# Short key tile split over the halves of a fast block product, in an attention and feed-forward kernel

## The chip, the core and the metric

The kernel runs on one core of a Trainium2 chip. The core has a matrix engine (TensorE, PE in the profile, with its weight loads as PEld), a vector engine (VectorE, DVE), a scalar engine (ScalarE, ACT), GpSimd (POOL) and SyncE (SP), which here only issues transfers. The engines run their own instruction queues in order and wait for one another through semaphores. The metric is the device time of one execution in microseconds, given as the median of several runs.

## The reference

For each of 4 batches there are 256 tokens of width 512 in x and 1601 rows of context of the same width. All data are fp32.

```python
xn = layernorm(x)
q = xn @ Wq + bq                     # 32 heads of 128
k, v = split(ctx @ Wkv + bkv)        # 8 key/value heads of 128; 4 query heads share one
attn = softmax(q @ k.T / sqrt(128))  # over the 1601 context rows
x = x + tanh(g_xattn) * ((attn @ v) @ Wo + bo)
h = layernorm(x)
x = x + tanh(g_ffn) * (h @ base_W.T + 2 * routed_lora(h))   # 8 experts, top 2, rank 16
```

1601 rows are twelve full tiles of 128 and a short one of 65. That short tile is what the change is about.

## The kernel before, in words

**Units.** The loop at the end of `flamingo_kernel` goes over batches `b` and key/value heads `h` (0 to 7) and, inside, over the two halves `l` of the 256 tokens. One such triple is a unit. `run_group(cur, prev)` writes the score matmuls of the current unit (`score_unit`, L799, tile `sc`, one matmul of 512 columns for each of 13 context tiles) alternately with the products of the previous unit's probabilities with the values (`av_unit`, L877, tile `av`). ScalarE copies each score tile from PSUM to SBUF (L806, tile `p`), VectorE keeps a running maximum (`fold`, tile `mx`, L731, L734 and L737) and later a running sum of the exponentials (tile `sm`).

**Softmax.** After a unit's scores, `softmax` reduces the maximum over partitions (`spread`: L769, L770, L750, L756, L757, L761, L764), then VectorE subtracts it from each pair of score tiles (L835) and ScalarE takes the exponential (L838). The first pair is the short tile alone. The first `av` matmul of the unit needs its exponential. The sums of the unit before are reduced by the same `spread` just ahead, and the result scales `av` to `oT` (L926, L930).

**Windows.** Between two units the function `window` puts other work on TensorE: query projections (`q_steps`, L480, `pq`), the output projection of a finished unit (`out_steps`, L942, `po`), key projections, value projections, context transposes (L226, `pt_ctx`) and the feed-forward steps. Each is a `Task`, a list of steps with costs, a time at which a step may start, and for some a due unit. A small clock in the kernel's own code (`clock`, `vec`, `act`, `later`, `pump`) estimates, with fixed figures for VectorE and ScalarE, when a result is ready; from these figures it decides at build time which step goes into which window and in which order VectorE and ScalarE get their instructions. The order of TensorE, VectorE and ScalarE is written out by hand this way (`manual_schedule`).

**Keys and values.** Keys and values of two heads are made together. `pair_steps` uses seven products of 2x2 blocks in place of eight: the context is cut into halves of 768 rows and each of the two heads' weights into blocks, and VectorE makes sums of context blocks (`ctx_sums`, L441, tile `T`, and `last_sums`, L452 and L456) once a batch. GpSimd makes the sums of the weights (`weight_sums`, L291). Each half is worked in two parts of 384 columns (`SUB`). The products of one part go to three PSUM banks (`pxk`, `pyk`, `pzk` for keys at L587, `pxv`, `pyv`, `pzv` for values at L598); between products ScalarE copies a bank out (L622, L626) and VectorE adds another bank to what was copied (L631). The short tile does not fit in the halves and has products of its own (L685, `ptk` and `ptv`).

The first pair of heads of every batch gets its keys by `plain_k_steps` (L512, `pk`): four chunks of 400 or 401 columns for each head, four matmuls a chunk. In batches 1 to 3 these steps lie in the last three windows of the batch before, and `last_sums` follows them.

**Buffers.** The context, its sums, the values and the weights of the output projection (`wo`) have one buffer each; the keys (`kT`) have three. `load_wo` for the next head is called in `out_steps` after the projection of a head's second half, since only then its buffer is free. The key and value weights share one buffer. SyncE issues the loads in the order of its queue.

Of the kernel before, what the change touches and what calls it, by code (L numbers as in the profile page):

```python
# [15 lines left out]
P = 128  # L16
# [11 lines left out]
def flamingo_kernel(  # L28
# [49 lines left out]

    nc = tc.nc
# [19 lines left out]
    n_chunks = -(-LK // 512)  # L99
    base, extra = divmod(LK, n_chunks)  # L100
# [3 lines left out]
    TAIL = 2 * HK  # L104
    chunks, s = [], 0
    for i in range(n_chunks):
        n = base + (1 if i < extra else 0)
        chunks.append((s, n))
        s += n
# [232 lines left out]
    xa_t, xnT_t, ctxT_t, T_t = {}, {}, {}, {}  # L342
# [40 lines left out]
    ctx_order += range(TAIL // P, KT)  # L383

    def ctx_steps(b):
# [9 lines left out]
        def begin():  # L395
            ctxT_t[b] = pool.tile([P, NC, LK], F32, tag="ctxT", name=f"ctxT_{b}", bufs=1)
            new_sums(b)

        def step(n):
            def run():  # L400
                i = ctx_order[n]
                if n + STAGE - 1 < KT:
                    load(n + STAGE - 1)
                turn_ctx(b, i, staged.pop(i))
                if n % 2 == 1 and i < TAIL // P:
                    ctx_sums(b, i * P - HK, P)
                if n == KT - 1:
                    done["ctx", b] = clock["now"] + 1000
            return NC * TR_COST, LAG_CTX, run, True
# [10 lines left out]
    def new_sums(b):  # L420
        t = pool.tile([P, 6 * HK + 2 * (LK - TAIL)], F32, tag="T", name=f"T_{b}", bufs=1)
        T_t[b] = (
            t[:, : 6 * HK].rearrange("p (n c k) -> p n c k", n=3, c=2),
            t[:, 6 * HK :].rearrange("p (c k) -> p c k", c=2),
        )

    def ctx_sums(b, s0, n):
# [3 lines left out]
        lo, hi = slice(s0, s0 + n), slice(HK + s0, HK + s0 + n)  # L431
# [12 lines left out]
    def last_sums(b):  # L444


        ct, tt = ctxT_t[b], T_t[b][1]
        for s0 in range(0, HK, SUB):
            b12, b22 = (ct[:, c : c + 2, HK + s0 : HK + s0 + SUB] for c in (0, 2))
# [6 lines left out]
            lambda: nc.vector.tensor_tensor(tt, ct[:, 2:4, TAIL:], ct[:, 0:2, TAIL:], ALU.subtract),  # L456
# [3 lines left out]
    def turn_ctx(b, i, src):  # L460
        transpose_rows(
            src,
            rows[i],
            ctxT_t[b][:, :, i * P : i * P + rows[i]],
            f"ctx_{b}_{i}",
            b > 0 or i % 2 == 1,
        )
# [37 lines left out]

    def plain_k_steps(b, h):

        def item(s, n):
            def run():
                pk = bank(f"pk_{b}_{h}_{s}")  # L510
                for c in range(NC):
# [3 lines left out]
                        ctxT_t[b][:, c, s : s + n],  # L515
# [3 lines left out]
                nc.scalar.activation(  # L519
                    kT_t[b, h][:, s : s + n], pk[:, :n], AF.Identity, bias=bias_of("k", h)  # L520
                )
                give(act(500))
            return NC * mm_cost(n), 0, run, True

        steps = [item(s, n) for s, n in chunks]
        return [(0, ("ctx", b), lambda: new_kT(b, h))] + steps

    def plain_v_steps(b, hp):
# [3 lines left out]
        def item(i):  # L532
# [3 lines left out]
            def run():  # L536
                w = w_t["v", b, hp]
                pv = bank(f"pv_{b}_{hp}_{i}")
                for j in range(n):
                    s = (i + j) * P  # L540
                    for c in range(NC):
# [3 lines left out]
                            ctxT_t[b][:, c, s : s + r],  # L545
# [12 lines left out]
    def pair_steps(kind, b, hp):  # L558
# [10 lines left out]
        def operand(i, c, s, n):  # L569
# [6 lines left out]
            if i == 3:  # L576
                return ct[:, 2 + c, HK + s : HK + s + n]
            if i == 7:
                return ct[:, c, HK + s : HK + s + n]
# [4 lines left out]
        def product(i, s, bk, first):  # L584
            if is_k:
                for c in range(2):
                    nc.tensor.matmul(  # L587
                        bk[:, :SUB],
                        a(SLOT[i], c),
                        operand(i, c, s, SUB),  # L590
# [16 lines left out]
        def place(f, half, s):  # L607

            if is_k:
                lo = half * HK + s  # L610
                return kT_t[b, h0 + f][:, lo : lo + SUB]
            lo = (half * HK + s) // P
            return v_t[b, hp][:, lo : lo + SUB // P, f, :]

        def seen(bk):
            if is_k:
                return bk[:, :SUB]
            return bk[:, :SUB].rearrange("p (t f) -> p t f", f=HDIM)

        def copy_to(f, half, s, bk):  # L620
            if is_k:
                nc.scalar.activation(  # L622
                    place(f, half, s), seen(bk), AF.Identity, bias=bias_of("k", h0 + f)
                )
            else:
                nc.scalar.copy(place(f, half, s), seen(bk))  # L626
            return act(470)

        def add_to(f, half, s, bk, ready=None):
            o = place(f, half, s)  # L630
            nc.vector.tensor_tensor(o, seen(bk), o, ALU.add)  # L631
            return vec(520, ready)

        def step(i, s):
# [3 lines left out]
            def run():  # L638
# [4 lines left out]
                product(i, s, bk, i in (1, 2, 7))  # L643
                if i == 1:
                    done[key] = done[nm, s, "x0"] = copy_to(0, 0, s, bk)
                elif i == 2:
                    give(add_to(0, 0, s, bk, max(clock["now"] + SEM, done[nm, s, "x0"])))
                elif i == 6:
                    done[key] = copy_to(1, 0, s, bk)
                elif i == 5:  # L650
                    done[key] = copy_to(1, 1, s, bk)
                    done[nm, s, "y"] = add_to(1, 1, s, banks[nm, s, "y"], done[key])
                elif i == 3:
                    give(copy_to(0, 1, s, bk))
                elif i == 4:
                    give(add_to(1, 0, s, bk))

            cost = 2 * (mm_cost(SUB) if is_k else SUB // P * BLOCK_COST)
# [5 lines left out]

        n = LK - TAIL

        def tail_cols(f):

            ct, tt = ctxT_t[b], T_t[b][1]
# [675 lines left out]
```

## Time and profile before

The median of three runs is 2690.46 us (2688.22 to 2691.63). One execution was profiled:

| | |
|---|---|
| profiled execution, its own time | 2691.11 us |
| its span, first to last instruction | 2689.3 us |
| mean granted TensorE clock | 0.995 |
| VectorE busy, ScalarE busy | 2151.5 us, 1199.3 us |
| scores, `sc`, L799 | 777.2 us in 1664 records |
| `av`, L877 | 769.5 us in 1640 records |
| plain keys, `pk`, L512 | 91.3 us in 256 records |
| short key tile, `ptk`, L685 | 24.7 us in 192 records |

How to read it: an fp32 matmul leaves two records. A row of the group list gives the line in the kernel, the engine, the operation, the tile written and the tiles read, the form (weight block, then partitions by columns), the count, the busy time and mean time of one, and the idle time of the engine before it with the one that released it. Matmul records overlap, so the time from one start to the next is shorter than a record. A row of the timeline gives start, length, engine, line, operation and how many records were merged.

### The profile page before, as it was taken

What the parts mean: (1) busy time and instruction counts of PE and PEld (TensorE: products, weight loads), DVE (VectorE), ACT (ScalarE), POOL (GpSimd) and SP (SyncE); (2) the same over time, 40 slices, a digit from 0 to 9 for tenths busy, and PEclk for the clock granted to TensorE, in tenths of its full rate; (3) what the DMA queues carried; (4) which work ended last, traced back from release to release, by engine and by line L of the source; (5) the groups of instructions that cost most, each with busy time, mean ns of one, the idle gap of its engine ahead of it and who ended that gap; (6) DMA issues with size and microseconds to landing.
All of it is one profiled execution on the core that took longest, in us unless ns stands there. A gap on an engine that the chain in (4) does not pass through costs nothing.

```text
span 2689.3 us, 25629 instructions
## 1 busy us (share of the span) xinstructions
PE 2634.7 (98%) x9323; PEld 1506.0 (56%) x9323; DVE 2151.5 (80%) x3299; ACT 1199.3 (45%) x1881; POOL 123.8 (5%) x130
## 2 busy tenths in 40 slices
PE   8999999999999999999999999999999999999997
PEld 6556555564655646556565555656556564565643
DVE  2688787888878878788888888878888788887885
ACT  2444444445444344445454444344544443443441
POOL 0001000000000002000000000000000010000000
PEclk9999999999999999999999999999999999999998
DMA  4101001121011011013010011011210110111000
GB/s 129 61 24 40 32 24 39 40 73 32 28 35 40 24 35 48 29 38 87 25 40 32 24 44 39 24 43 35 66 40 24 32 47 20 39 43 34 22 16 8
DMA packets 78263, 104.72 MB, mean 39 GB/s; under 512 B 3324, under 2 KB 36140, under 8 KB 78136
## 3 DMA queue, kind: packets, MB, share of 16 engines
q1 hardware_dynamic: 76728, 102.01, 12.1%
q8 instruction: 73, 1.20, 0.2%
q0 software_dynamic: 272, 0.53, 0.1%
q10 hardware_dynamic: 1136, 0.55, 0.1%
q14 instruction: 54, 0.44, 0.1%
HBM read 100.98 MB, written 2.10 MB: 38 GB/s over the span
## 4 chain that ended last, share of the span: by engine, by line
PE 83%; DVE 13%; ACT 3%; issue 1%; DMA 0%; SPq 0%; DVEq 0%; ACTq 0%
PE sc L799 23%; PE av L877 22%; PE po L942 8%; PE pq L480 7%; PE pxk L587 5%; PE pk L512 3%; PE pxv L598 3%; PE pyv L598 2%; DVE sm L737 2%; DVE mx L737 2%; PE pyk L587 2%; ACT p L806 2%; PE pzk L587 1%; PE ptv L685 1%; PE py L994 1%
## 5 line engine op out<-in xcount | busy, mean ns | idle before, releaser
L799 PE MATMUL sc<-qT,kT 128*128 128x512 f32 (+1 forms) x1664 | 777.2, 593 | 2.3 <-ACT qT L487 2.3
L877 PE MATMUL av<-p,v 65*128 65x512 f32 x1640 | 769.5, 595 | 7.2 <-ACT p L838 7.2
L806 ACT COPY p<-sc 65x512 f32<-65x512 f32 x820 | 463.3, 588 | 559.5 <-PE sc L799 402.0
L877 PEld LDWEIGHTS av<-p,v 65*128 65x128 f32 x1640 | 310.7, 191 | 392.2 <-issue 368.0
L799 PEld LDWEIGHTS sc<-qT,kT 128*128 128x128 f32 (+1 forms) x1664 | 307.7, 186 | 382.6 <-issue 361.3
L838 ACT ACTIVATE p<-p 65x512 f32<-65x512 f32 x442 | 425.8, 992 | 166.7 <-DVE p L835 161.3
L737 DVE TENSOR_TENSOR mx<-mx,p 128x1024 f32<-128x1024 f32 x252 | 308.8, 1225 | 236.8 <-ACT p L806 231.9
L835 DVE TENSOR_TENSOR p<-p,res_mx 65x512 f32<-65x512 f32 x442 | 480.6, 1137 | 0.3
L737 DVE TENSOR_TENSOR sm<-sm,p 128x1024 f32<-128x1024 f32 x252 | 313.7, 1245 | 8.8 <-DVE sm L734 0.5
L942 PE MATMUL po<-wo,oT 128*128 128x512 f32 x512 | 232.5, 597 | 2.8 <-ACT oT L930 2.8
L480 PE MATMUL pq<-xnT,wq 128*128 128x256 f32 x1024 | 234.1, 380 | 0.0
L480 PEld LDWEIGHTS pq<-xnT,wq 128*128 128x128 f32 x1024 | 192.7, 190 | 45.7 <-issue 19.4
L942 PEld LDWEIGHTS po<-wo,oT 128*128 128x128 f32 x512 | 96.7, 192 | 105.8 <-issue 93.0
L622 ACT ACTIVATE kT<-pxk,biasT 128x384 f32<-128x384 f32 x96 | 55.6, 579 | 220.6 <-PE pxk L587 220.6
L731 DVE TENSOR_TENSOR mx<-p,p 128x1024 f32<-128x1024 f32 x63 | 77.2, 1225 | 81.6 <-ACT p L806 81.4
L291 POOL TENSOR_TENSOR wv<-wv 128x256 f32<-128x256 f32 x60 | 60.0, 1021 | 1766.5 <-DMA wv<-in_L_xattn_Wkv_dram 1552.1
L626 ACT COPY v<-pxv 128x384 f32<-128x384 f32 x120 | 56.5, 476 | 151.1 <-PE pxv L598 150.9
L487 ACT ACTIVATE qT<-pq,biasT 128x256 f32<-128x256 f32 x128 | 60.5, 473 | 124.2 <-PE pq L480 123.7
L512 PE MATMUL pk<-ctxT,wk 128*128 128x400 f32 (+1 forms) x256 | 91.3, 507 | 2.4 <-DVE ctxT L231 1.4
L598 PE MATMUL pxv<-wv,T 128*128 128x128 f32 x720 | 90.2, 275 | 0.0
L598 PEld LDWEIGHTS pxv<-wv,ctxT 128*128 128x128 f32 x720 | 85.2, 192 | 7.2 <-issue 6.9
L598 PE MATMUL pxv<-wv,ctxT 128*128 128x128 f32 x720 | 87.7, 275 | 0.0
(157 smaller groups left out, 2378.3 us busy)
## 6 DMA issues: line engine op xcount, KB each, us to landing
wq<-in_L_xattn_Wq_dram SPq DMA_DIRECT2D x32, 1024.0 KB, 5.4
wo<-in_L_xattn_Wo_dram SPq DMA_DIRECT2D x32, 1024.0 KB, 5.3
ctx<-in_ctx_dram SPq DMA_DIRECT2D x48, 256.0 KB, 2.6
wk<-in_L_xattn_Wkv_dram SPq DMA_DIRECT2D x30, 256.0 KB, 3.1
wv<-in_L_xattn_Wkv_dram SPq DMA_DIRECT2D x30, 256.0 KB, 3.0
xa<-in_x_dram SPq DMA_DIRECT2D x4, 512.0 KB
out_dram<-y SPq DMA_DIRECT2D x8, 256.0 KB, 2.1
base<-in_L_ffn_base_W_dram SPq DMA_DIRECT2D x4, 256.0 KB, 9.4
```

Source lines behind the costliest of these rows:

```text
L480: nc.tensor.matmul(pq[:, :L], w_t["q", b, h][:, c, g * HDIM : (g + 1) * HDIM], xnT_t[b][:, c, :], start=(c == 0), stop=(c == NC - 1),)
L512: nc.tensor.matmul(pk[:, :n], w_t["k", b, h // 2][:, raw_slot(h % 2, c), c % 2, :], ctxT_t[b][:, c, s : s + n], start=(c == 0), stop=(c == ...
L587: nc.tensor.matmul(bk[:, :SUB], a(SLOT[i], c), operand(i, c, s, SUB), start=first and c == 0, stop=c == 1, skip_group_check=True,)
L598: nc.tensor.matmul(bk[:, t * HDIM : (t + 1) * HDIM], operand(i, c, s + t * P, P), a(SLOT[i], c), start=first and t == 0 and c == 0, stop=c ...
L731: nc.vector.tensor_tensor(acc, p[first], p[first + 1], op)
L737: nc.vector.tensor_tensor(acc, acc, p[j], op)
L799: nc.tensor.matmul(sc[:r, :], kT_t[b, h][:, i * P : i * P + r], qT_t[b, h][:, :, l * P : (l + 1) * P], start=True, stop=True,)
L806: nc.scalar.copy(p[:r, k, :], sc[:r, :])
L835: nc.vector.tensor_tensor(p, p, m, ALU.subtract)
L838: nc.scalar.activation(p, p, AF.Exp, scale=scale)
L877: nc.tensor.matmul(av, v_t[b, h // 2][:r, i, h % 2, :], p_t[key][j][:r, k, :], start=(j == 0 and k == 0), stop=(j == NPAIR - 1 and k == le ...
L942: nc.tensor.matmul(po, oT_t[key][:, g, :], w_t["o", b, h][:, g, :], start=(g == 0), stop=(g == G - 1),)
```

## The change

The short tile of 65 rows is split in 32 (`REST0`) and 33 (`HT`) rows, each put in front of one half of the context, and the shorter one is padded with a column of zeros by GpSimd. A half thus has 33 + 768 columns (`HW`), and the parts of a half are 417 and 384 columns (`parts_of_half`). The keys need no products of their own for the short tile; the values keep theirs, from a tile `rest` that holds the short tile's transpose. ScalarE copies the two pieces from `rest` to the context tile. The keys of the tile land in the middle of `kT`, so a result of 417 columns in the first half goes out in two copies or adds (384 and 32 columns, `key_places`), and scores find a tile by `key_col`.

The first pair of heads of batches 1 to 3 uses `pair_steps` too, so its weights get their sums, and `last_sums` runs right after the last transpose of a batch's context. Batch 0 keeps `plain_k_steps`, with the new parts as chunks, and loads the short tile first.

The figures that the planning clock uses for VectorE and ScalarE are changed in `copy_to`, `add_to`, `fold`, `spread` and `softmax`, and three small copies move from one piece of `spread` to the piece before. Two small tiles get two buffers instead of four.

```diff
-    TAIL = 2 * HK
-    chunks, s = [], 0
...
+    REST = rows[-1] if FULL < KT else 0
+    REST0 = REST // 2
+    HT = REST - REST0
+    HW = HT + HK
+
+    parts_of_half = [(0, HT + SUB)] + [(HT + s, SUB) for s in range(SUB, HK, SUB)]
...
+    def key_col(i):
+
+        return HK if i == FULL else i * P + (REST if i * P >= HK else 0)
+
+    def new_ctx(b):
+        ctxT_t[b] = pool.tile([P, NC, 2 * HW], F32, tag="ctxT", name=f"ctxT_{b}", bufs=1)
+        rest_t[b] = pool.tile([P, NC, REST], F32, tag="rest", name=f"rest_{b}", bufs=1)
+        if REST0 < HT:
+
+            nc.gpsimd.memset(ctxT_t[b][:, :, REST0:HT], 0.0)
...
-                if n % 2 == 1 and i < TAIL // P:
-                    ctx_sums(b, i * P - HK, P)
+                if n % 2 == 1 and i < FULL:
+                    ctx_sums(b, ctx_col(i) - HW, P)
+                if i == FULL:
+                    ctx_sums(b, 0, HT)
                 if n == KT - 1:
-                    done["ctx", b] = clock["now"] + 1000
+                    last_sums(b)
...
+        rest = rest_t[b]
+        transpose_rows(src, REST, rest, f"ctx_{b}_{i}", True)
+        nc.scalar.copy(ctxT_t[b][:, :, :REST0], rest[:, :, :REST0])
+        act(300)
+        nc.scalar.copy(ctxT_t[b][:, :, HW : HW + HT], rest[:, :, REST0:])
+        act(300)
...
+    def key_places(b, h, half, s, n):
+
+
+        k = kT_t[b, h]
+        if half == 1:
+            return [(k[:, HK + REST0 + s : HK + REST0 + s + n], 0, n)]
+        if s > 0:
+            return [(k[:, s - HT : s - HT + n], 0, n)]
+        full = [(k[:, : n - HT], HT, n - HT)]
+        return full + [(k[:, HK : HK + REST0], 0, REST0)] if REST0 else full
...
+        def copy_to(f, half, s, n, bk):
+            for dst, src in places(f, half, s, n, bk):
+                m = src.free_size()
+                if is_k:
+                    nc.scalar.activation(dst, src, AF.Identity, bias=bias_of("k", h0 + f))
+                    t = act(190 + m)
+                else:
+                    nc.scalar.copy(dst, src)
+                    t = act(90 + m)
+            return t
+
+        def add_to(f, half, s, n, bk, ready=None):
+            for dst, src in places(f, half, s, n, bk):
+                nc.vector.tensor_tensor(dst, src, dst, ALU.add)
+                t = vec(140 + 1.04 * src.free_size(), ready)
+            return t
...
-        left = [7 * HK // SUB + (n > 0)]
-        parts = [[step(i, s) for i in (1, 2, 6, 7, 5, 3, 4)] for s in range(0, HK, SUB)]
-        if n:
+            cols = parts_of_half
+        else:
+            new_v(b, hp)
+            cols = [(HT + s, SUB) for s in range(0, HK, SUB)]
+        parts = [[step(i, s, n) for i in (1, 2, 6, 7, 5, 3, 4)] for s, n in cols]
+        if REST and not is_k:
...
-                return 1910
+                return 1930
...
             )
-
-        def whole():
             for a in range(1, 4):
                 nc.vector.tensor_copy(q[:32, a, :], q[32 * a : 32 * a + 32, 0, :])
+
+        def whole():
...
-            (690, quadrants),
-            (1300, whole),
+            (1240, quadrants),
+            (1070 if after is not None else 800, whole),
...
-                later(
-                    "sum", "v", 1220, ("exp", key, j), lambda j=j: sum_piece(key, j), ("sum", key, j)
-                )
+                first = NPAIR - FULL // 2
+                ns = 0 if j <= first else 1230 if j > first + 1 else 1970 if first else 1230
+                later("sum", "v", ns, ("exp", key, j), lambda j=j: sum_piece(key, j), ("sum", key, j))
...
+    first_order = [*range(FULL, KT), *range(FULL)]
...
-                if coming[0] == b:
-                    steps = sum(pair_steps("k", *coming), [])
-                else:
-                    steps = sum((plain_k_steps(b + 1, f) for f in range(2)), [])
-                    steps.append((0, 0, lambda b=b: last_sums(b + 1)))
+                steps = sum(pair_steps("k", *coming), [])
                 tasks.append(Task(steps, (hi | 1) * NL + NL - 1, True))
...
                 load_pair("k", *coming)
-                if coming[0] == b:
-                    weight_sums("k", *coming)
+                weight_sums("k", *coming)
```

## The prediction

> **What bounds the kernel now.** I read the page's engine shares first.
>
> ```profile
> PE 2634.7 (98%) x9323; PEld 1506.0 (56%) x9323; DVE 2151.5 (80%) x3299; ACT 1199.3 (45%) x1881; POOL 123.8 (5%) x130
> ```
>
> TensorE is the bound, and its chain is 83% of the span. But matmul records overlap, so I take its pace from starts in the timeline of one window between two attention units:
>
> ```profile
> 353.30 1.45 PE L587 MATMUL pxk<-ctxT,wk 128*128 128x384 f32 x4
> 354.59 1.45 PE L587 MATMUL pyk<-T,wk 128*128 128x384 f32 x4
> 355.88 1.45 PE L685 MATMUL ptk<-ctxT,wk 128*128 128x65 f32 x12
> 357.17 0.61 PE L685 MATMUL ptk<-T,wk 128*128 128x65 f32 x4
> 357.61 3.67 PE L480 MATMUL pq<-xnT,wq 128*128 128x256 f32 x16
> ```
>
> Every fp32 matmul is two records (passes). A block product of 384 columns takes 354.59 - 353.30 = 1.29 us, 0.3225 a pass; the short key tile takes 357.61 - 355.88 = 1.73 us for only 65 columns. A second look, at the last windows of batch 0, shows who sets TensorE's start:
>
> ```profile
> 641.23 3.60 PE L877 MATMUL av<-p,v 128*128 128x512 f32 x8
> 644.67 5.54 PE L512 MATMUL pk<-ctxT,wk 128*128 128x401 f32 x16
> 650.05 3.60 PE L942 MATMUL po<-wo,oT 128*128 128x512 f32 x8
> 653.48 2.85 PE L512 MATMUL pk<-ctxT,wk 128*128 128x400 f32 x8
> 656.17 2.74 PE L799 MATMUL sc<-qT,kT 128*65 128x512 f32 x6
> 658.74 1.02 PE L877 MATMUL av<-p,v 65*128 65x512 f32 x2
> ```
>
> po has 0.429 a pass (3.43/8), pk of 400 columns 0.336. The first av at 658.74 needs this unit's softmax, which VectorE and ScalarE make meanwhile:
>
> ```profile
> 642.05 1.23 DVE L737 TENSOR_TENSOR mx<-mx,p 128x1024 f32<-128x1024 f32 x1 [1.07 <-ACT p L806]
> ...
> 652.79 0.69 DVE L835 TENSOR_TENSOR p<-p,res_mx 65x512 f32<-65x512 f32 x1
> ```
>
> ```profile
> 653.56 1.28 ACT L838 ACT_TABLE_LOAD   x1 [2.71 <-DVE p L835]
> 654.85 0.63 ACT L838 ACTIVATE p<-p 65x512 f32<-65x512 f32 x1
> ```
>
> The exponential ends at 655.48, 3.26 us before av needs it. So TensorE is the bound only where its window work covers the softmax; that cover is what the change touches.
>
> **Part 1: the key tile in two halves, three pairs in each of four batches, 12.** Removed: the tail, 1.73 us. Added: 14 matmuls (28 passes) grow from 384 to 417 columns. The slope is (0.429 - 0.3225)/128 = 0.83 ns a column, so 33 x 0.83 = 0.0275 us a pass, 0.77 us. Gain 0.96 us a pair, 11.5 us in all, all on TensorE's chain.
>
> VectorE gets two small adds a pair (32 columns; bounds 0.15, a one-column add, and 0.29, the 130-column one; I take 0.19) and 33 more columns in one (0.03). ScalarE's two key tail copies (0.31 each) become two 32-column ones behind the 384-column copy (0.58): 0.9 us, under the product that lies between (1.40); without that cover 0.3 us a pair. The adds are hidden where the softmax is covered. In all VectorE gains some 18 us over the kernel (18 adds of 0.53 for the new pairs, 30 small ones, nine 66-element sums near 0.22), 81% of the span instead of 80%.
>
> **Part 2: block products for the first pair of batches 1 to 3.** Plain: 64 passes x 0.336 = 21.5 us. Blocks: 28 x 0.350 + 28 x 0.3225 = 18.8 us. Gain 2.7 us, three times: 8.0. Batch 0 stays plain (32 x 0.350 + 32 x 0.3225 = 21.5): nothing. VectorE's last sums of the context (1.0 + 0.95 + 0.3 us, and three small ones of 0.2) now run before these products instead of after; the first two products and two pq items, 6 us, lie between the last transpose and the first product that reads them: hidden.
>
> **Part 3: the new figures move the order.** They run nothing by themselves; I compared the built instruction orders.
>
> *In-batch waits go.* The wait list has
>
> ```profile
> PE pyv L598 <- DVE v L631: 16.1, 15, 2.0
> ```
>
> These are waits of 1.9 us after tight windows (exponential ready 0.1 us ahead) and of 0.4 after looser ones (2 us or more ahead). The window at the end of a pair grows from 11.2 us (2 x 1.29 + 1.73 + 2 x 1.73 + 3.43) to 12.0, and one sum of 1.24 us leaves the softmax queue behind it. So most go to 0.4: 6 x 1.5, and 1 us at the exponentials, 10 us. Bounds: 0 (nothing moves) and 13.
>
> *The softmax at the batch edge loses its cover.* At the unit (head 7, first half) of batches 0, 1, 2 the window holds in the new order two products of 417 (2 x 1.40) and two of 384 (2 x 1.29), 5.38 us, where it held 11.50: po of head 6's second half is put one window later. Cover from the last score: 8 av passes 3.43 + 5.38 + 6 score passes 2.58 = 11.39 us, before 17.51. The softmax grows: before, from the last score's end (641.23) to 655.48, 14.25 us. Now two sums of 1.2 stand between last maximum and spread, and three key adds (0.53, 0.19, 0.53, overlapped 1.2) before the first subtraction: 14.25 + 2.4 + 1.2 = 17.85. So av waits 17.85 - 11.39 = 6.45 us. Bounds: 4.5, if the sums slip in while ScalarE copies scores, and 7.5, with the copy queue of ScalarE behind. VectorE has done the earlier maxima by then and waits for the last scores, as before (1.07 us in the row at 642.05), so no backlog adds to it. All scores of the next unit beyond the first three queue behind this av.
>
> *The load of wo loses its cover.* The window of (head 7, second half) becomes three products, po of head 6, one product, po of head 7. wo has one buffer: head 7's load starts when head 6's last po pass is done.
>
> ```profile
> 653.67 0.38 SPq L295 DMA_DIRECT2D wo<-in_L_xattn_Wo_dram  x1
> ```
>
> ```profile
> DMA to landing us min/median/max: 5.0/5.3/9.4
> ```
>
> The issue comes 0.19 us after po's end (653.48), landing 5.3 later: 5.49. Before, a whole unit of 22 us lay between; now one product of 1.29 does. Wait 4.2 us; bounds 3.9 and 8.1 from min and max. Ahead of it on SP's queue stand the context loads and wq of the next batch, whose buffers have long been free; behind it wv, needed 29 us later. On VectorE the add of po waits with it, and the next unit's subtractions behind that, but after po TensorE still has a product, four pq (6.9 us) and the scores (2.6), against 3 us of queue: hidden. POOL has a four-column fill more (0.1 us) and four weight sums of 1.0 for the first pair, 22 us ahead of need.
>
> *The clock.* Long waits cost more than themselves:
>
> ```profile
> 90.97:94.38 3.41, 0.32 (x3) 0.08 (x1) 3.26 (x5) 2.18 (x3) 0.00 (x0) 1.00 0.26 77
> 94.38:97.79 3.41, 3.12 (x7) 1.92 (x8) 0.66 (x2) 2.13 (x3) 0.00 (x0) 0.50 0.02 5
> 97.79:101.20 3.41, 3.41 (x5) 1.35 (x4) 3.41 (x4) 1.57 (x2) 0.00 (x0) 0.50 0.26 79
> ```
>
> ```profile
> 2606.58:2609.99 3.41, 1.15 (x3) 0.32 (x3) 3.41 (x5) 1.69 (x2) 0.00 (x0) 1.00 0.93 300
> 397.90:401.31 3.41, 1.69 (x16) 1.50 (x15) 3.26 (x12) 0.48 (x1) 0.00 (x0) 1.00 0.00 0
> ```
>
> (Columns: length, then busy time of PE, PEld, DVE, ACT, POOL; granted clock, DMA share, GB/s.) The clock changes on a grid of 3.41 us. A window busy 0.32 us is followed by two at half clock; one busy 1.15 us (34%) by one, to 2613.41; one busy 1.69 us (50%) by none. A wait of 4.2 us leaves some window busy under 38% wherever it lies: one to two windows at half, less what falls in the wait, 0.6 to 3.4 us lost; I take 1.9. The 6.45 us wait empties a window: two at half, 1.9 to 3.4; I take 2.6. The Trainium skill, "TensorE: Matmul & The Clock Gate", Part 1, asks for a wholly idle window of about 3.4 us before the half rate, and for one busy window after it. By it the first wait costs 1.7 and the second, which holds a whole window in (4.2 - 3.4)/3.4 of its positions, 0.4. An edge is 6.45 + 2.6 + 4.2 + 1.9 = 15.15 us by the rows, 12.75 by the page (8 us over the kernel instead of 15). The row at 2606.58 contradicts the page's whole window, so I take the rows.
>
> **Start and end.** The start loads the short tile first; the first keys need tiles 12, 0, 1, 2 (898 KB) instead of 0 to 3 (1024 KB), against one more transpose and two copies on ScalarE: within 1 us either way, taken as 0. The end is ordered as before: 0.
>
> **Sum.** -11.5 - 8.0 - 10 + 3 x 15.15 = +16, on the profiled span of 2689.3 us: 2705.3. That execution took 2691.11, 1.8 of it outside the span; the median 2690.46 lies 0.65 below. Measured from the median: 2706.
>
> **The rivals.**
> *All hidden* (TensorE at 98% speaks for it, the 11.39 us of cover against): -29.5, 2661. Chance 0.04.
> *Only the load waits, the softmax keeps its cover*, which ends on the faster side: the edge is then 6.1 us, -29.5 + 18.3 = -11, 2679. The place is the queue between the last maximum and the first subtraction of (head 7, first half). It decides from 9.8 us of wait and clock an edge (29.5/3), so if av waits under about 2.5 us, which needs a queue of under 14 us. The 14.25 us shown before the added five instructions speak against. Chance 0.10.
> *Only the softmax waits, the load is hidden anyway*: 3 x 9.05 - 29.5 = -2, 2688. For it: the load would have to start before po of head 6 ends, and the one buffer forbids it. Chance 0.09, with half-clock smaller than thought included.
> *Both wait, clock at its worst, in-batch waits stay*: 3 x (7.5 + 3.4 + 4.2 + 3.4) - 21.5 = +34, 2724. For it: the clock's grid lies by chance. Chance 0.11.
> Forecast: 0.66, own range 2697 to 2715.
>
> **How the numbers follow.** Two thousandths, 5.4 us, is about what a measurement tells from no change. Faster: 0.04 + 0.10. Same: 0.09 and 0.01 of the forecast's low end. Slower: 0.65 + 0.11. The range leaves out 2661, 2679 and the upper half of 2724's case: 2684 to 2717.
>
> **What would show it.** Right: ptk rows gone, half the block products at 417 with 0.35 a pass; before av of (head 7, first half) near 3 edges an idle PE of 5 to 7 us, released by the exponential; before po of head 7 some 4 us with the load's landing behind it; half-clock windows after both; pyv waits down to about 6 us. Wrong: no half clock between 120 and 2600 us, or a wait of po under 2 us, or pyv waits as before.

## The result, and the profile after

The changed kernel takes 2725.68 us (median of four runs, 2721.54 to 2726.78), the kernel before 2690.47 beside it: 1.0129 times, 95% interval 1.0112 to 1.0147. It is slower, as forecast, but by 35 us instead of 16, and above the stated range of 2684 to 2717. The profiled span grew from 2689.3 to 2723.8 us, by 34.5.

The engine shares of the changed kernel's page:

```profile
PE 2633.5 (97%) x9107; PEld 1486.4 (55%) x9107; DVE 2181.4 (80%) x3355; ACT 1207.4 (44%) x1898; POOL 165.7 (6%) x146
```

216 passes fewer on TensorE, and almost the same busy time. GpSimd's busy time went from 123.8 to 165.7 us for 16 instructions more. The twelve new sums of key weights, which the prediction has at 1.0 us each, are 13 of these 42 us. Another 28 are the same 60 sums of value weights as before (60.0 us, now 88.4), and no step of the prediction accounts for them.

To see where the span went I took the distance from each TensorE start to the next and split it into the median for its shape (work) and the rest (stall):

| us | before | after | difference | forecast |
|---|---|---|---|---|
| work | 2612.1 | 2592.5 | -19.6 | -19.5 |
| stall ahead of pyv | 18.5 | 20.3 | +1.8 | -10 |
| three batch edges, without pyv | 2.5 | 52.3 | +49.8 | +45.5 |
| start (110 us), end, the rest | 47.3 | 50.1 | +2.8 | 0 |
| sum | 2680.4 | 2715.2 | +34.8 | +16 |

The difference of 0.3 to the span lies outside the first and last product. Runs below with the same products have 2589.7 to 2592.5 us of work, so the work row is sure to some 3 us and its agreement to a tenth is chance. Two thirds of the miss is the second row. The changed kernel's list of waits (total, times, longest) has all three large ones:

```profile
PE av L912 <- ACT p L873: 27.2, 6, 6.5
PE pyv L640 <- DVE v L676: 18.3, 12, 2.2
PE po L977 <- DMA wo<-in_L_xattn_Wo_dram: 12.4, 3, 4.2
```

The edge of batch 0 in TensorE's timeline, where the prediction put the two waits:

```profile
640.99 1.56 PE L629 MATMUL pxk<-ctxT,wk 128*128 128x417 f32 x4
...
645.08 1.45 PE L629 MATMUL pzk<-ctxT,wk 128*128 128x384 f32 x4
646.38 2.74 PE L834 MATMUL sc<-qT,kT 128*65 128x512 f32 x6
655.64 2.08 PE L912 MATMUL av<-p,v 65*128 65x512 f32 x2 [6.53 <-ACT p L873]
...
682.30 3.60 PE L977 MATMUL po<-wo,oT 128*128 128x512 f32 x8
685.74 1.45 PE L629 MATMUL pxk<-ctxT,wk 128*128 128x384 f32 x4
691.37 5.37 PE L977 MATMUL po<-wo,oT 128*128 128x512 f32 x8 [4.18 <-DMA wo<-in_L_xattn_Wo_dram]
```

From start to start, the av stalls 6.7 us at each edge (6.45 forecast) and the second po 4.2 to 4.4 (4.2 forecast). The clock in windows on its own grid (length, busy time of PE, PEld, DVE, ACT, POOL, granted clock, DMA share, GB/s):

```profile
647.94:651.35 3.41, 1.17 (x3) 0.19 (x1) 3.20 (x6) 2.89 (x5) 0.00 (x0) 1.00 0.00 0
651.35:654.76 3.41, 0.00 (x0) 0.00 (x0) 3.25 (x12) 0.30 (x1) 0.00 (x0) 0.50 0.00 0
654.76:658.18 3.42, 2.54 (x3) 1.18 (x4) 3.42 (x4) 2.58 (x3) 0.00 (x0) 0.50 0.00 0
658.18:661.59 3.41, 3.41 (x5) 1.35 (x4) 3.41 (x4) 3.18 (x4) 0.00 (x0) 0.50 0.00 0
```

```profile
688.89:692.31 3.42, 0.94 (x3) 0.50 (x4) 1.49 (x3) 0.00 (x0) 0.00 (x0) 1.00 0.50 195
692.31:695.73 3.42, 3.42 (x6) 1.33 (x5) 0.00 (x0) 0.00 (x0) 0.00 (x0) 0.50 0.00 0
695.73:699.14 3.41, 3.41 (x13) 2.26 (x12) 2.37 (x4) 0.63 (x1) 0.00 (x0) 1.00 0.00 0
```

Three windows at half clock after the first wait, one after the second. Over 655.64 to 661.59 half of 5.95 us is lost (3.0), over 692.31 to 695.73 half of 3.42 (1.7): 4.7 us at this edge. At the other two edges the grid lies otherwise: more of the three windows falls behind the av wait, two windows at half fall around the second po, and the loss is 6.0 and 5.9. Mean 5.5, forecast 4.5. At the second edge the clock stays at half behind a window in which TensorE was busy from end to end, and the third edge has the same:

```profile
1320.37:1323.78 3.41, 3.41 (x5) 1.35 (x6) 3.41 (x4) 2.94 (x3) 0.00 (x0) 0.50 0.00 0
1323.78:1327.19 3.41, 3.41 (x6) 1.35 (x5) 3.41 (x4) 2.35 (x3) 0.00 (x0) 0.50 0.00 0
```

### The profile page after: what moved, and what is told of

The parts are those of the page before. It is cut to its first block, busy times and chain, and to the rows that moved or that the text cites. A ratio compares the mean times of both kernels' runs of the same rounds, so it can differ in the third digit from the quotient of the medians.

```text
span 2723.8 us, 25225 instructions
## 1 busy us (share of the span) xinstructions
PE 2633.5 (97%) x9107; PEld 1486.4 (55%) x9107; DVE 2181.4 (80%) x3355; ACT 1207.4 (44%) x1898; POOL 165.7 (6%) x146
## 3 DMA queue, kind: packets, MB, share of 16 engines
q1 hardware_dynamic: 76728, 102.01, 11.8%
## 4 chain that ended last, share of the span: by engine, by line
PE 78%; DVE 16%; ACT 3%; issue 1%; DMA 1%; SPq 0%; ACTq 0%; DVEq 0%
PE av L912 21%; PE sc L834 20%; PE po L977 8%; PE pq L504 8%; PE pxk L629 5%; DVE p L870 3%; PE pyk L629 3%; DVE sm L772 3%; PE pyv L640 3%; ACT p L841 2%; DVE mx L772 2%; PE pxv L640 2%; PE pzk L629 1%; PE ptv L727 1%; PE py L1029 1%
## 5 line engine op out<-in xcount | busy, mean ns | idle before, releaser
L870 DVE TENSOR_TENSOR p<-p,res_mx 65x512 f32<-65x512 f32 x442 | 498.3, 1180 | 0.0
L977 PE MATMUL po<-wo,oT 128*128 128x512 f32 x512 | 239.5, 612 | 15.2 <-DMA wo<-in_L_xattn_Wo_dram 12.4
L291 POOL TENSOR_TENSOR wv<-wv 128x256 f32<-128x256 f32 x60 | 88.4, 1492 | 1738.5 <-DMA wv<-in_L_xattn_Wkv_dram 1737.3
L667 ACT ACTIVATE kT<-pxk,biasT 128x384 f32<-128x384 f32 (+2 forms) x150 | 75.8, 526 | 264.4 <-PE pxk L629 264.4
L291 POOL TENSOR_TENSOR wk<-wk 128x256 f32<-128x256 f32 x60 | 70.5, 1195 | 523.4 <-DMA wk<-in_L_xattn_Wkv_dram 397.0
L984 DVE SCALAR_TENSOR_TENSOR xa<-po,gates,xa 128x512 f32<-128x512 f32 x64 | 47.9, 749 | 62.5 <-PE po L977 62.4
L629 PE MATMUL pxk<-ctxT,wk 128*128 128x417 f32 (+1 forms) x240 | 90.5, 499 | 0.0
```

Of the source, the lines that this page charges most:

```text
L291: nc.gpsimd.tensor_tensor(w[:, out_], w[:, x_], w[:, y_], op)
L629: nc.tensor.matmul(bk[:, :n], a(SLOT[i], c), operand(i, c, s, n), start=first and c == 0, stop=c == 1, skip_group_check=True,)
L870: nc.vector.tensor_tensor(p, p, m, ALU.subtract)
L977: nc.tensor.matmul(po, oT_t[key][:, g, :], w_t["o", b, h][:, g, :], start=(g == 0), stop=(g == G - 1),)
```

## Why the waits of pyv stayed: reading the two traces

pyv waits for VectorE's adds of the products before it, which stand in VectorE's queue behind the maximum of the scores. A row is from here on one unit's run of alternating score and av products. In all 27 places of the two traces where pyv waits, its stall is the time from the start of the row's last score record to the end of the last maximum, less 2.9 to 3.0 us (or less 5.6 in the first row of a batch). So the question is what makes VectorE late by the end of a row. In the row after a key pair of the changed kernel, VectorE and GpSimd:

```profile
1031.04 0.56 DVE L676 TENSOR_TENSOR kT<-pyk,kT 128x384 f32<-128x384 f32 x1 [0.54 <-PE pyk L629]
1031.52 6.82 DVE L870 TENSOR_TENSOR p<-p,res_mx 128x1024 f32<-128x1024 f32 x5
1038.26 1.74 DVE L766 TENSOR_TENSOR sm<-p,p 128x1024 f32<-128x1024 f32 x1
```

```profile
1034.58 6.01 POOL L291 TENSOR_TENSOR wv<-wv 128x256 f32<-128x256 f32 x4 [112.47 <-DMA wv<-in_L_xattn_Wkv_dram]
```

Five subtractions take 6.82 us and the first sum 1.74; alone they take about 5.75 and 1.21 (shown below). Beside GpSimd's four sums of the value weights two of the subtractions and the first sum are longer by 0.53 us each, and the short sum behind them by 0.41: 2.0 us. GpSimd's sums themselves take 6.0 us, where four alone take 2.9. The sums start when the weights land, the load starts when the last key product has read the shared buffer, and that product has moved. SyncE and TensorE, a row of the kernel before:

```profile
1172.79 0.92 SPq L277 DMA_DIRECT2D wv<-in_L_xattn_Wkv_dram  x2
```

```profile
1172.11 0.61 PE L685 MATMUL ptk<-T,wk 128*128 128x65 f32 x4
1172.55 3.67 PE L480 MATMUL pq<-xnT,wq 128*128 128x256 f32 x16
1176.06 3.60 PE L942 MATMUL po<-wo,oT 128*128 128x512 f32 x8
1179.50 1.45 PE L799 MATMUL sc<-qT,kT 128*65 128x512 f32 x3
```

and of the changed kernel:

```profile
1031.08 0.92 SPq L277 DMA_DIRECT2D wv<-in_L_xattn_Wkv_dram  x2
```

```profile
1026.12 3.60 PE L977 MATMUL po<-wo,oT 128*128 128x512 f32 x8
1029.55 1.45 PE L629 MATMUL pyk<-T,wk 128*128 128x384 f32 x4
1030.84 2.74 PE L834 MATMUL sc<-qT,kT 128*65 128x512 f32 x6
```

Before, the tail was the last reader, four pq and po lay behind it, and the load was issued 6.7 us ahead of the scores. Now the last product stands behind po and the load is issued 0.2 us after they start. The twelve rows inside a batch are all alike in this (6.7 to 7.0 us ahead before, 0.2 to 0.6 us after now). The sums move from the spread of the maximum, where most of them fell, onto the subtractions. The Trainium skill, "SBUF — State Buffer", section "SBUF: two separate sides", says that a VectorE instruction with two SBUF inputs and a GpSimd instruction that reads SBUF share one pair of ports, and that the one that starts first holds it for its whole length while the other is blocked. The subtraction is such an instruction, and the 1.75 us against 1.22 agree in kind; no trace shows the ports. The prediction did not draw on that page. In the row shown VectorE ends its last maximum 4.25 us after the last score record starts.

## The experiments

**Are the new figures what moved the order?** The planner's figures for ScalarE and VectorE were set back, the two parts of the key products kept.

```diff
-            (1240, quadrants),
-            (1070 if after is not None else 800, whole),
+            (690, quadrants),
+            (1300, whole),
...
-                ns = 0 if j <= first else 1230 if j > first + 1 else 1970 if first else 1230
+                ns = 1220
```

(and 1910, 470 and 520 for the first fold, the copies and the adds. The three small copies stay in their new piece of `spread`, and so does the figure for batch 0's plain keys.)

> The changed kernel with every figure of the planner for VectorE and ScalarE set back to those of the kernel before (470 and 520 for the copies and adds of a product, 690 and 1300 for the spread, 1220 for each sum, 1910 for the first fold). The prediction laid the moved order to the figures. If they are its cause, the two waits at each of the three batch edges go (6.7 and 4.3 us, and about 5 us of half clock), and the in-batch waits stand near 16 us: 2690 - 19.7 = 2671. If the products themselves (fourteen items of even cost, no short tile at the end) move the order, the windows stay and so does the time: 2721 to 2728.

Measured: 2743.36 us, 1.0198 (1.0182 to 1.0213). Neither: the time went up by 18. Its waits of TensorE:

```profile
PE av L912 <- ACT p L873: 31.8, 7, 7.9
PE pyv L640 <- DVE v L676: 25.5, 12, 2.4
PE po L977 <- DMA wo<-in_L_xattn_Wo_dram: 12.0, 3, 4.0
```

All three large waits are there without the new figures, so the reshaped products are enough to move the windows, and with them the figures give 18 us back. The prediction had laid the moved order to the figures. The new figures with the old products were not run, nor was either part of the products alone.

**GpSimd's sums taken away.** `raw_in_place` loads raw weights into the places of the sums; everything else keeps its place. This kernel leaves the sums of the value weights out and so computes something else.

```diff
                 load_pair("v", *coming)
-                weight_sums("v", *coming)
+                raw_in_place(*coming)
```

> The changed kernel without GpSimd's weight sums for the value weights of fifteen pairs: raw weights are loaded into their places, so these sums are left out of what is computed; the order on TensorE, VectorE and ScalarE is unchanged. Theory (GpSimd's sums now run beside VectorE's subtractions and slow three or four of them by 0.53 us each, since the last key product, which frees the weights' buffer, was moved behind po): VectorE ends its last maximum some 2 us sooner in the unit before each value pair, the twelve waits of pyv fall from 20 us in all to under 4, and the kernel to about 2709. Rival (VectorE is late for its own added sums and adds): the waits and the time stay, 2723 to 2728.

Measured: 2701.13, 1.0043 (1.0027 to 1.0060), 24.5 us less than the changed kernel. VectorE in the row that answers to the one above:

```profile
1020.57 5.76 DVE L879 TENSOR_TENSOR p<-p,res_mx 128x1024 f32<-128x1024 f32 x5
1026.24 1.22 DVE L775 TENSOR_TENSOR sm<-p,p 128x1024 f32<-128x1024 f32 x1
```

The subtractions are 1.06 us shorter for five, the sum 0.52, and the short sum 0.41. VectorE now waits 0.47 us ahead of the first maximum, so 1.5 of the 2.0 us should be left at the row's end, and the end of the last maximum, counted from the start of the last score record, does come down from 4.25 to 2.74. In other rows it came from 5.30 to 3.18, where three subtractions and a sum had been slowed, 2.12 us in all. The stall of pyv went from 20.3 to 1.4 us in all. That is the theory, and somewhat more than its number. The other 5.6 us are small differences, most of them at the edges: with the same two waits the grid of the clock fell better there, and the half clock cost 4.4 us an edge instead of 5.5.

**The same sums made late in the kernel before.** One short product holds the key weights to the end of the window.

```diff
+            if h % 2 == 1 and l == NL - 1 and coming is not None and coming[0] == b:
+                hold = bank(f"hold_{hi}")
+                nc.tensor.matmul(
+                    hold[:, :P], w_t["k", *coming][:, A11, 0, :], ident, start=True, stop=True
+                )
```

> The kernel before with one useless product of 128 columns (0.22 us) that reads the key weights at the end of the last window of each of the twelve pairs within a batch, so that the value weights' load, and GpSimd's sums behind it, start some 10 us later, as in the changed kernel. Theory: the sums fall on the subtractions, slow three or four of them by 0.53 us, and the waits of pyv grow by 1 to 2 us in each of the twelve: 2690 + 2.6 + 12 to 24 = 2705 to 2717. Rival (the place of the sums does not matter): 2690 + 2.6 = 2693.

Measured: 2693.52, 1.0011 (1.0002 to 1.0021), the rival's number. The slowing is there in its VectorE timeline:

```profile
1017.16 6.83 DVE L835 TENSOR_TENSOR p<-p,res_mx 128x1024 f32<-128x1024 f32 x5
1023.92 1.75 DVE L731 TENSOR_TENSOR sm<-p,p 128x1024 f32<-128x1024 f32 x1
1025.70 1.10 DVE L734 TENSOR_TENSOR sm<-sm,p 65x512 f32<-65x512 f32 x1
1026.86 1.23 DVE L731 TENSOR_TENSOR mx<-p,p 128x1024 f32<-128x1024 f32 x1
```

but it does not reach pyv in full. The same row of the kernel before has the idle time that takes it up:

```profile
1018.48 5.75 DVE L835 TENSOR_TENSOR p<-p,res_mx 128x1024 f32<-128x1024 f32 x5
1024.15 1.21 DVE L731 TENSOR_TENSOR sm<-p,p 128x1024 f32<-128x1024 f32 x1
1025.40 1.10 DVE L734 TENSOR_TENSOR sm<-sm,p 65x512 f32<-65x512 f32 x1
1027.48 1.23 DVE L731 TENSOR_TENSOR mx<-p,p 128x1024 f32<-128x1024 f32 x1 [0.98 <-ACT p L806]
```

VectorE waited 0.98 us for scores ahead of the first maximum, and in the late version it starts these subtractions 0.4 us sooner after the first score: the added product delays the scores by 0.2 us, and the sums no longer stretch the short subtraction ahead. What remains is 0.15 to 0.3 us more of pyv's wait in six of the twelve rows.

In the other six pyv waited 0.2 us less than before, and they show a second way in which the two engines meet. There too the first of GpSimd's sums began beside the subtractions, but it was GpSimd that was held:

```profile
208.71 5.88 POOL L291 TENSOR_TENSOR wv<-wv 128x256 f32<-128x256 f32 x1 [137.02 <-DMA wv<-in_L_xattn_Wkv_dram]
205.99 6.88 DVE L835 TENSOR_TENSOR p<-p,res_mx 128x1024 f32<-128x1024 f32 x6
```

One sum took 5.88 us (5.3 to 5.9 in the six rows), and the six subtractions, at 1.21 us each, lost nothing; only the short sum and the first maxima behind them were longer. The kernel before has such a sum too, 7.51 us long, beside the five subtractions of its row above. In all fifteen rows of the changed kernel with such sums subtractions were slowed. What decides which engine is held was not found. So a late sum is not enough by itself: it has to slow the subtractions, and that costs where VectorE has no slack ahead of the first maximum. In the row shown of the changed kernel that first maximum follows with no idle time, and without the sums it has only 0.47 us.

**The weight sums made once.** They depend on the pair of heads and not on the batch. GpSimd makes each of the eight sets one time and keeps it in device memory; later batches load seven blocks instead of four. All of the reference is computed.

```diff
+        if (kind, hp) in kept:
+            nc.sync.dma_start(w, kept[kind, hp])
+            w_t[kind, b, hp] = w
+            return
...
+        if b < B - 1:
+            kept[kind, hp] = dram.tile([P, 7, 2, HDIM], F32, tag=f"kept_{kind}_{hp}", name=f"kept_{kind}_{hp}")
+            nc.gpsimd.dma_start(kept[kind, hp], w)
```

> The changed kernel with the weight sums made once: they depend on the pair alone, not on the batch, so GpSimd makes each of the eight sets one time, writes the block of seven to device memory, and later batches load it (896 KB instead of 512). All of the reference is computed. Theory (GpSimd's sums slow the subtractions and so hold pyv): the nine waits of pyv in batches 1 to 3 go, those of batch 0 (2.35, 2.35, 1.82) stay: 20.3 to about 7, and about 1 us beside key pairs: 2725.7 - 14 = 2712. Rival (the longer load is late in place of the sums): 2722 or slower.

Measured with the changed kernel: 2709.66, 1.0075 (1.0060 to 1.0090), 16 us less. Its wait list has

```profile
PE pyv L652 <- DVE v L688: 6.5, 3, 2.2
```

three waits, those of batch 0, where the sums are still made; the nine of the later batches are gone. The stall of pyv fell from 20.3 to 7.7 us.

> The kernel before with the weight sums made once. There the sums fall on the spread of the maximum, where they stretch small copies by 0.2 to 0.5 us each, about 1 us a unit. Theory: that lag too reaches pyv; the nine waits of batches 1 to 3, 8 us in all, fall by about 1 us each or to nothing: 2690 - 5 = 2685. Rival (only sums on the subtractions matter): 2689 to 2691.

Measured with the kernel before: 2687.34, 0.9990 (0.9980 to 0.9999). Of the three rows inside each later batch, the last maximum came 1.1 us sooner in the first (4.84 to 3.72 us after the last score record); in the others it did not move, and the stall of pyv fell by 3.3 us. The sums cost the kernel before about 3 us of pyv's stall in these batches, where they cost the changed one 13.

**The half clock, by useless work in the waits.** Seven products of 512 columns at the first wait, five ahead of the second po. First they were put at the end of the window, ahead of the scores:

```diff
                 window(now)
+                if (h, l) == (NKV - 1, 0):
+                    fill = bank(f"fill_{b}")
+                    for _ in range(7):
+                        nc.tensor.matmul(fill, ident, base_t[:, 0, :], start=True, stop=True)
...
             po = bank(f"po_{nm}")
+            for _ in range(5 if (h, l) == (NKV - 1, 0) and b < B - 1 else 0):
+                nc.tensor.matmul(po, ident, base_t[:, 0, :], start=True, stop=True)
```

> The changed kernel with useless products at each of the three batch edges: seven of 512 columns (6.0 us of TensorE) at the end of the window of head 7's first half, five (4.3 us) ahead of po of head 7's first half. Theory (the two waits are lack of cover, and the half clock follows from the idle time): the av wait falls from 6.7 to 0.7 us, the po wait from 4.3 to near 0, the half clock of about 4.7 us an edge goes: 2725.7 - 14 = 2711 to 2713, faster for 31 us of added work. Rival 1 (waits are filled, but the half clock does not come from the idle time): 2724 to 2728. Rival 2 (the waits move behind the added work): 2725.7 + 31 = 2757.

Measured: 2725.58, 1.0132 (1.0117 to 1.0147), as rival 1 has it, but for another reason. The wait of po went; that of av fell only from 6.7 to 3.4 us, and half clock followed. ScalarE's timeline shows why:

```profile
655.90 0.58 ACT L841 COPY p<-sc 128x512 f32<-128x512 f32 x1 [0.27 <-PE sc L834]
656.38 0.72 ACT L965 ACTIVATE oT<-oT,biasT 128x512 f32<-128x512 f32 x1
657.13 1.28 ACT L873 ACT_TABLE_LOAD   x1
658.42 2.52 ACT L873 ACTIVATE p<-p 65x512 f32<-65x512 f32 x3
```

The scores had been delayed by the filler, their copies stand ahead of the exponential on ScalarE, and the first exponential ended 17.3 us after the window's start, in the changed kernel 14.6. So the number for the half clock could not be read from it, and the seven products were moved behind the first three score tiles.

> As the run with useless products, but the seven for head 7's first half stand behind the first three score products instead of ahead of them, so that ScalarE copies these scores when it did. In the run before, the exponential came 3.4 us late behind the copies on ScalarE. Theory (waits are lack of cover, half clock follows from idle time): the av wait falls from 6.7 to 0.7 us, po's to near 0, no half clock at the edges: 2725.7 - 14 = 2712. Rival (the half clock does not follow from these waits): 2724 to 2728.

Measured: 2711.11, 1.0082 (1.0066 to 1.0099), 14.6 us faster than the changed kernel with 31 us of work added. TensorE at this edge:

```profile
647.71 6.17 PE L1184 MATMUL fill<-base_t,ident 128*128 128x512 f32 x14
654.39 1.12 PE L912 MATMUL av<-p,v 65*128 65x512 f32 x2 [0.51 <-ACT p L873]
```

At the three edges no window is at half clock any more. The waits are lack of cover, and the half clock follows from the idle time.

**The load of wo alone.** po of head 7's first half behind the four pq (the part left out of the cut sets the gate after the last of them).

```diff
...
+        first = ("gate", b) if (h, l) == (NKV - 1, 0) and b < B - 1 else ("oT", key)
-        return [(G * mm_cost(D), ("oT", key), project, True)] + (
+        return [(G * mm_cost(D), first, project, True)] + (
```

> The changed kernel with po of head 7's first half put behind the four pq at each batch edge, 8.6 us of other products after po of head 6 instead of 1.3, against 5.5 us for the load of wo. Theory: the wait for the load and its half clock go, 4.3 + 1.75 us at each of three edges, 18 us: about 2707; the softmax's wait of 6.7 us stays. Rival (what stands behind po, the sum into xa and the feed-forward's first steps, is late in its place): 2718 to 2728.

Measured: 2700.60, 1.0041 (1.0026 to 1.0056), 25 us less. The wait for wo is gone, that of av stays at 6.5. Some 7 us of the 25 are not the load's: the planner, with its clock moved, also laid the later batches out otherwise, and the stall of pyv fell from 20.3 to 13.1.

**The edge's window mended.** Eight key products may go into the window of head 7's first half, which brings po of head 6 back into it.

```diff
             t.credit = t.cost() / (later_ + 1) if later_ > 0 else NEVER
+            if t.chain and later_ > 0 and now % (NKV * NL) == (NKV - 1) * NL:
+                t.credit = sum(s[0] for s in list(t.steps)[:8]) - 1
```

> The changed kernel with one thing more: the key products may take eight items in the window of head 7's first half, which brings po of head 6 back into it. The window is 13.97 us instead of 5.38, the cover from the last score 13.97 + 6.0 = 20 us against a chain of 17.85, and a unit of 22 us lies between the two po again. Theory: both waits and the half clock behind them go at each edge, about 16 us three times: 2676 to 2680, the in-batch waits as in the changed kernel. Rival (the short window only moves to head 7's second half, now 11.6 us, and the softmax waits there): half of it, 2695 to 2705.

Measured: 2690.14, 1.0001 (0.9992 to 1.0009): 35.5 us less, where 46 to 50 were expected. po no longer waits. The av still does, 2.8 us, for the same cause as with the filler: later scores, and the exponential behind their copies. Hence the next edit, the exponential first.

```diff
             if cur is not None and j < NPAIR:
+                if prev is not None and j == 0 and prev[1:] == (NKV - 1, 0) and prev[0] < B - 1:
+                    force(("exp", prev, 0))
```

> As the run with the edge's window filled, and the first exponential of head 7's first half put ahead of the next unit's score copies in ScalarE's order. There the exponential stood behind three copies and its table load, 2.8 us late, and half clock followed. Theory: the wait falls to about 0.4 us and the half clock goes, some 5 us at each of three edges: 2690 - 15 = 2675, faster than both kernels. Rival (the first maximum of the next unit is late in its place, since its copies now wait): 2684 to 2692.

Measured: 2681.69, 0.9968 (0.9956 to 0.9981). The wait of av and its half clock are gone. Of the 15 us expected 8.5 came: in the traces an edge cost 4.7 us of stall and now 1.2, so only 10.5 us were to be had, and pyv takes 4.2 back, most of it because it waits anew, 1.2 us, in the first row of each later batch, where VectorE is now later.

**A second way to free the value weights sooner** was to take a tenth more key products in the first windows of a pair, so that the last comes ahead of po.

```diff
+            elif t.chain and later_ > 0 and now % (NKV * NL) < (NKV - 2) * NL:
+                t.credit *= 1.1
```

(with the edge's eight products, and leave to wait for them in the edge's windows.)

> The changed kernel with the edge's window filled as before (eight key products and po of head 6 in the window of head 7's first half) and, in the batch, a tenth more of the key products taken in each of the first two windows of a pair, so that the last of them is ahead of po at the pair's end (window 10.75 us). Theory: the value weights are loaded some 4 us sooner, GpSimd's sums fall on the spread of the maximum instead of the subtractions, and the pyv waits fall from 20 us to under 6; the edges cost 4 to 5 us each as with the window alone: 2690 - 15 = 2675, faster than both. Rival (the shorter last window of 10.75 us leaves the softmax late, as windows near 11.2 us did in the kernel before): 2686 to 2692.

Measured: 2734.26, 1.0167 (1.0152 to 1.0182). The stall of pyv is zero, and both edge waits are gone, but the time is 44 us above that of the edge's window alone. TensorE's wait list has

```profile
PE pyk L629 <- DVE kT L676: 32.9, 9, 3.7
PE pxk L629 <- issue: 19.0, 3, 6.3
```

The last product needs an add that stands behind the spread in VectorE's queue, and pulled ahead of po it waits 3.7 us for it; in the changed kernel po stands in between. At the edges early products wait up to 6.3 us. The profile names no releaser for this; VectorE's sums of the context, which run until about then, are the likely one.

**Edge and sums together.**

> The two together: window of the edge filled, exponential ahead of the copies, weight sums made once. If the effects are separate they add: 2675 - 14 = 2661, 1.1% faster than the kernel before. If they share a cover, 2665 to 2675.

Measured: 2667.41, 0.9914 (0.9899 to 0.9928). It beats the kernel before by 23 us and the changed one by 58. The gains nearly add: 44.0 for the edge and 16.0 for the sums would be 60.0 if separate, and 58.3 came.

## Why the prediction was wrong, point by point

*Parts 1 and 2* were right: -19.5 forecast, -19.6 of work measured (sure to some 3 us), 350 ns a pass at 417 columns as interpolated.

*"In-batch waits go"* failed: -10 forecast with bounds 0 and -13, +1.8 measured. The longer window did what was said of it once the sums were away: 1.4 us of stall is left, less than the 0.4 us a wait that was forecast. What was left out is the load behind the last key product. The prediction followed the moved products on TensorE, and of GpSimd it asked only whether the sums would be in time for their user, not what runs beside them. The value weights' load slid by 7 us past po, its sums met VectorE's subtractions, and 18.9 us of stall came back. That is 11.8 of the 18.5 us by which the span's growth was missed.

*"The new figures move the order"* named a cause that is not needed. The figures are worth -18 us on top of the reshaped products; the windows at the edge lose their cover with the old figures too. The sum did not rest on it, since the order was read from the built kernel.

*The batch edge* was right in mechanism and place. The waits measured 6.7 and 4.3 us for 6.45 and 4.2 (the upper bound of the second, 8.1, should be 8.3 by its own numbers). The term mis-sized was the half clock: 5.5 us an edge for 4.5, 3 us over the kernel. The longer wait has three windows at half, of which 1.7 to 2.1 fall behind it, and the shorter one has two at two edges of three. A good part of this is where the grid lay: with the same two waits an edge lost 4.4 us to the half clock in the run without sums and 4.7 in the changed kernel with sums made once, near the forecast. The estimate from the Trainium skill's rule ("TensorE: Matmul & The Clock Gate", Part 1) was 2.1. Here windows busy for 1.17 and 0.94 us were followed by half clock, and so was one busy for 2.54 us at half clock (74%), behind which the rule would expect the full rate if it counts as busy; at the other two edges even a window busy throughout was.

*The rest*, 2.8 us of stall at the start, the end and between, was taken as nothing.

Of the rivals, *both wait, clock at its worst, in-batch waits stay*, 2724 us at a chance of 0.11, is nearest to what came, but with pyv held by another cause than it gave. That its figure lies within 2 us of the measured time is luck: its edges cost 18.5 us each where 16.6 were measured, and pyv and the rest made up for it. Its sum also takes off 21.5 us where parts 1 and 2 alone are 19.5, so with all in-batch waits staying it should have read +36, 2726. The range left out its upper half, and the time lay in it.

## What to carry to other kernels

When an instruction is moved, follow what it releases as well as what it needs: the buffer, the load that was waiting for that buffer, the work behind the load, and what that work now runs beside. An engine that is 5% busy can lengthen the whole if it slows another at the one place without slack; the slack ahead of the next wait decides how much of such a slowing arrives (in the rows shown, 1.5 us of 2.0 in one kernel and 0.3 of 2.0 in the other). Work that depends on fewer loop indices than it is done for is best made once, which took the neighbour away altogether.

## What the hardware showed that was not expected

- A subtraction of 128x1024 with two SBUF operands took 1.75 us beside GpSimd's sums and 1.22 alone; the sums of 128x256 took 1.7 us beside it and 0.73 alone. There both lose. In other rows of the kernel before and of its late version the subtractions kept their 1.21 us, and one sum took 5.3 to 7.5 us.
- Useless products in a wait made the kernel faster: 31 us of work added, 14.6 us gained, since the clock stayed whole.
- TensorE's clock fell to half after windows that were busy for 34% and 28% of 3.41 us. Behind windows at half clock that were busy for 74%, and in two places throughout, it was still at half; behind another that was busy throughout it was full again.
